# State space stage of a fused layer kernel: scan tiles of four states by 32 channels

## The chip, the cores and the metric

The kernel runs on one core of one Trainium2 chip. The metric is the device time of one execution, in microseconds (us); lower is better. The median of the runs before the change is 4260.15 us (4258.0 to 4260.63, 3 runs).

## The reference

Six parts follow each other on `x` of shape 16 x 512 x 256 (batch, time, features): a quantised feed-forward half step, a selective state space step, the feed-forward half step again, a LoRA half step, a causal attention, a LoRA half step. The change is in the state space step alone, which is this, for each batch:

```python
xz = layernorm(x) @ W_in;  x, z = split(xz)              # 512 x 512 each
x  = silu(conv(x) + conv_b)                              # 4 taps along time, per channel; called u below
proj = x @ W_x;  dt_low, Bm, Cm = proj[:16], proj[16:32], proj[32:]
dt = softplus(dt_low @ W_dt + b_dt);  A = -exp(A_log)    # A: 512 channels x 16 states
h_t = exp(dt_t * A) * h_(t-1) + (dt_t * x_t) * Bm_t      # 512 channels x 16 states, 512 times
y_t = sum over states of h_t * Cm_t
out = ((y + x * D) * silu(z)) @ W_out
```

## The kernel before

The state space stage is `mamba_phase`. Time lies along the free axis, channels along the 128 partitions. A batch is 32 steps (`STEPS`): four chunks `c` of 128 channels, and in each chunk eight steps `k` of two states. I write s0 to s31 for the steps of a batch, s = 8c + k. One step does this:

- POOL (`make_bx`, called two steps ahead): `bx` = dt*u times a row of B. Three buffers.
- ACT (`factors`, called one step ahead): two Exp of 511 elements into `da`, a PSUM tile, two buffers.
- VectorE (DVE): one `tensor_tensor_scan` over 128 x 1024 elements (both states in a row) into `h`. `h` lies in PSUM with one buffer; for two `k` of eight (`other`) it lies in SBUF as `hs`, and POOL makes `g` instead of DVE.
- DVE or POOL: `g` = h times a row of C.
- TensorE (PE, `accumulate`): adds `g` of both states to `y`, one PSUM bank, by two 128x128 matmuls with the identity; the first of a chunk adds u*D before. Float32 matmuls of 512 columns are two instructions each.
- At the end of a chunk, `finish_mult` on DVE multiplies `zs` (silu of z) by `y`.

The rows of B and C come over DRAM: the projection goes to `bd`, and `fetch` loads one `bc` tile of 128 x 2048 for each `k` with a broadcast over the 128 partitions (1 MB, eight a batch, in chunk 3 of the batch before). `dt` and `dt*u` stay in SBUF, in tiles of their own.

While a batch is scanned, a Python generator, `prepare(b + 1)`, makes the next batch's inputs, one piece per step: transposes, input projections, conv taps, `w_x`, `w_dt`, z. Its PSUM tile `mm` has one buffer, so that a piece goes PE, ACT, PE, ACT. The conv works on `stacks` (`xs`): ACT copies a projected chunk to `xp`, one DMA stores it to DRAM (`xc`), four DMAs load it to 32 partitions each (`xs`), each shifted by one time step, and `taps(c)` folds them by matmuls of 128x32 into four groups of 32 output partitions. For chunk 3 of the next batch, `taps(3)` is PE's piece of s13 and its bias (`to_u(3)`) ACT's piece of s14.

Each engine runs its instructions in the order written (`keep_in_program_order`); DMAs all go on SP's queue, in an order that the framework's scheduler decides, and SP waits there for the buffer and the data of one DMA before it looks at the next. The framework gives DMAs eight semaphores in turn, so a DMA also waits for the eighth before it.

Of the kernel before, what the change touches and what calls it, by code (L numbers as in the profile page):

```python
# [16 lines left out]
P = 128  # L17
# [8 lines left out]
NS = 16  # L26
# [10 lines left out]
def macaron_kernel(  # L37
# [365 lines left out]
    def mamba_weights(mw):  # L403
        w = {}
        w["in"] = mw.tile([P, KD, 2 * DI], F32, name="w_in")
        nc.sync.dma_start(out=w["in"], in_=W_in.rearrange("(k p) f -> p k f", p=P))

        w_x = mw.tile([P, NDC, P], F32, name="w_x")
        nc.gpsimd.memset(w_x, 0.0)
        wx_src = W_x.rearrange("(c p) f -> p c f", p=P)  # L410
        for i in range(3):
            nc.sync.dma_start(
                out=w_x[:, :, 32 * i : 32 * i + 16],
                in_=wx_src[:, :, 16 * i : 16 * (i + 1)],
            )
# [13 lines left out]
        a_neg = mw.tile([P, NDC, NS], F32, name="a_neg")  # L429
        nc.sync.dma_start(out=a_neg, in_=A_log.rearrange("(c p) n -> p c n", p=P))  # L430
# [12 lines left out]
        nc.gpsimd.tensor_tensor(fold, ident[:, :32], ident[:, 32:64], op=ALU.add)  # L443
        for i in range(2, 4):
            nc.gpsimd.tensor_tensor(
                fold, fold, ident[:, 32 * i : 32 * i + 32], op=ALU.add
            )
        for c in range(NDC):
            nc.gpsimd.tensor_scalar(
                w["dskd"][:, c, :], fold, w["dsk"][:, c : c + 1], None, op0=ALU.mult  # L450
            )
            for i in range(4 * c, 4 * c + 4):
                nc.gpsimd.tensor_scalar(
                    w["cwd"][:, i, :], fold, cw[:, i : i + 1], None, op0=ALU.mult
                )

        w["taps"] = mw.tile([P, NDC, DCONV], F32, name="ct")
        nc.sync.dma_start(out=w["taps"], in_=conv_wT.rearrange("(c p) k -> p c k", p=P))
        w["xp"] = []
        for i in range(2):  # L460
            w["xp"].append(mw.tile([P, SEQ], F32, name=f"xp{i}"))

        w["xT"] = mw.tile([P, KD, SEQ], F32, name="xT")
        return w

    def mamba_phase(w, src, dst):
        with tc.tile_pool(name="m1", bufs=1) as m1, tc.tile_pool(
# [11 lines left out]
            def pool(out, in0, in1, op):  # L479
                tc.keep_in_program_order(nc.gpsimd.tensor_tensor(out, in0, in1, op=op))  # L480
# [9 lines left out]

            w_in, w_x, w_dt, w_out = w["in"], w["x"], w["dt"], w["out"]
            a_neg, dskd, cwd, xps = w["a"], w["dskd"], w["cwd"], w["xp"]
            NP = NS // 2
            STEPS = NDC * NP


# [13 lines left out]
                stacks.append(t)  # L510

            state, xns, xos, zss, rows, norms, bds = {}, {}, {}, {}, {}, {}, {}


            h0 = ps_h.tile([P, 2, SEQ], F32, name="h", tag="h")
# [17 lines left out]
                    )  # L533
                return p

            def fetch(b, k):


                if b < NB:
                    bc = m2.tile([P, 2, 2, SEQ], F32, name="bc", tag="bc", bufs=NP)  # L540
                    nc.sync.dma_start(
                        out=bc, in_=bds[b][k : k + 1].to_broadcast([P, 2, 2, SEQ])
                    )
                    rows[b, k] = bc

            def load(b):

# [53 lines left out]
            def prepare(b):  # L601
# [109 lines left out]
                bd = md.tile([NP, 2, 2, SEQ], F32, name="bd", tag="bd")  # L711
                for i in range(2):
                    nc.sync.dma_start(
                        out=bd.rearrange("k n i s -> (k n) i s")[:, i, :],
                        in_=proj[32 + 32 * i : 32 + 32 * i + NS, :],
                    )
                bds[b] = bd
                dts, dtus = [], []

                def to_dtu(h):  # L720
                    for j in range(2):
                        pool(dtus[h][:, j, :], dts[h][:, j, :], us[h][:, j, :], ALU.mult)

                for h in range(2):
                    dt = m2.tile([P, 2, SEQ], F32, name="dt", tag="dt", bufs=3)
                    dtu = m2.tile([P, 2, SEQ], F32, name="dtu", tag="dtu", bufs=3)
                    dts.append(dt)
                    dtus.append(dtu)
                    for j in range(2):
                        c = 2 * h + j  # L730
                        p = mm()
# [3 lines left out]
                        )  # L735
                        yield
                        act(
                            dt[:, j, :], p, AF.Identity, bias=w["bdt"][:, c : c + 1]
                        )
                        if h and j == 0:  # L740
                            to_dtu(0)
                    yield
                    act(dt, dt, AF.Softplus)
                state[b] = (us, dts, dtus)
                scale = norm_scale(b + 1)
                next(scale, None)
                yield "scan"
# [58 lines left out]
            def make_bx(t):  # L806
                b, c, k = where(t)
                if b < NB:
                    bx = m2.tile([P, 2, SEQ], F32, name="bx", tag="bx", bufs=3)
                    dtu = state[b][2][c // 2][:, c % 2 : c % 2 + 1, :]  # L810
                    pool(
                        bx, dtu.to_broadcast([P, 2, SEQ]), rows[b, k][:, :, 0, :], ALU.mult
                    )
                    bxs[t] = bx

            def accumulate(b, c, k, g):
                if k == 0:
                    ys.append(ps_y.tile([P, SEQ], F32, name="y", tag="y"))
                    u = state[b][0][c // 2][:, c % 2, :]
                    for i in range(0, P, 32):  # L820
                        pe(
                            ys[0][i : i + 32, :], lhsT=dskd[i : i + 32, c, :],
                            rhs=u[i : i + 32, :], start=True, stop=False,
                        )
                for j in range(2):
                    pe(
                        ys[0], lhsT=ident, rhs=g[:, j, :], start=False,
                        stop=(k == NP - 1 and j == 1),
                    )
                if k == NP - 1:  # L830
                    done.append((b, c, ys.pop()))

            def flat(t):
# [3 lines left out]
            for n, got in enumerate(rest):  # L837
# [3 lines left out]
                        pass  # L841
                if got:
                    break
            for k in range(NP):
                fetch(0, k)
            spare.clear()
            for t in range(2):
                make_bx(t)
            def factors(t):

                b, c, k = where(t)
                if b < NB:
                    for j in range(2):
                        n = 2 * k + j
                        act(
                            das[t % 2][:, j, 1:], state[b][1][c // 2][:, c % 2, 1:],
                            AF.Exp, scale=a_neg[:, c, n : n + 1],
                        )

            factors(0)  # L860
            due = {}
            for t in range(STEPS * NB):
                b, c, k = where(t)
                s = t % STEPS
# [3 lines left out]
                make_bx(t + 2)  # L868
                factors(t + 1)

                other = k % 4 == 1
                if other:
                    h = m2.tile([P, 2, SEQ], F32, name="hs", tag="hs", bufs=1)
                else:
# [4 lines left out]
                ))  # L879


                for args in reversed(due.pop(t, ())):
                    accumulate(*args)
                if s == 8:
                    load(b + 2)
                if 16 <= s < 24:
# [1 line left out]

                for _ in range(2 if t < 8 else 1):
                    next(rest if t < 4 else ahead, None)  # L890
                g = m2.tile([P, 2, SEQ], F32, name="g", tag="g", bufs=4)
                C = rows[b, k][:, :, 1, :]
# [4 lines left out]
                due.setdefault(t + 1 + other, []).append((b, c, k, g))  # L897
# [7 lines left out]
            for args in due.pop(STEPS * NB):  # L905
                accumulate(*args)
# [829 lines left out]
```

## Time and profile before

| | |
|---|---|
| median of 3 runs | 4260.15 us |
| span of the profiled execution | 4259.0 us |
| state space stage, first to last scan | 617.5 to 2429.3 us of the span, 512 scans |
| DMA share in this stage | 0.39 to 0.49 |
| PE, DVE, ACT, POOL busy, window 1000 to 1100 us | 89.4, 93.0, 73.6, 88.0 us |

The page gives the span of the profiled execution; the runs' times lie about 1 us above it. The page's columns: a group of instructions is given by its line, engine and operation, with the tiles it writes and reads, the number, the busy time, the mean of one, and the idle time just before them with what ended it. A matmul is recorded with its weight load (PEld) apart. PEclk is the share of full clock that TensorE was granted. Shares over the whole span mix stages; this stage is 43% of it.

### The profile page before, as it was taken

The page shows a single profiled execution, that of the slowest core. Times are in us where ns is not written, and L with a number is a line of the kernel's source. Part 1 is how long each engine was busy: PE and PEld are TensorE (multiplying, and loading weights), DVE is VectorE, ACT ScalarE, POOL GpSimd, SP SyncE. Part 2 cuts the span into 40 slices and gives each one's busy share as a digit, 9 for nine tenths or more (in the row PEclk, how much of TensorE's full clock was granted, in tenths as well). Part 3 has the DMA queues.
Part 4 walks back from the last instruction along what each step waited for, and adds up shares of the span by engine and source line. Part 5 has one row for each costly group of instructions (what it writes and reads, how often), then busy time and mean ns, then how long its engine had stood idle before and what let it go on. Part 6 is the DMA issues. An engine that isn't in the chain of part 4 may idle for free.

```text
span 4259.0 us, 50441 instructions
## 1 busy us (share of the span) xinstructions
PE 3903.6 (92%) x17986; PEld 2129.9 (50%) x17986; DVE 3751.8 (88%) x4970; ACT 2284.9 (54%) x3463; POOL 1877.2 (44%) x1653
## 2 busy tenths in 40 slices
PE   6999977988899888888888799999999999999989
PEld 4676632333333333333333366666755555555547
DVE  9999858999999999999999899998878888888766
ACT  4444336667767676676777344443524444444434
POOL 1000027888888898888988600000301111111121
PEclk9999999999999999999999999999999999999999
DMA  4000023444444444444443020000000000000002
GB/s 143 16 16 15 20 100 104 132 122 134 139 144 144 144 143 144 134 135 133 139 138 120 11 109 1 1 1 1 13 21 20 19 17 18 19 20 14 21 11 70
DMA packets 120605, 303.00 MB, mean 71 GB/s; under 512 B 25297, under 2 KB 45330, under 8 KB 103970
## 3 DMA queue, kind: packets, MB, share of 16 engines
q1 hardware_dynamic: 120354, 299.78, 22.4%
q8 instruction: 142, 2.33, 0.2%
q14 instruction: 109, 0.89, 0.1%
HBM read 238.63 MB, written 44.30 MB: 66 GB/s over the span
## 4 chain that ended last, share of the span: by engine, by line
PE 66%; DVE 14%; POOL 12%; ACT 5%; issue 2%; DMA 1%; SPq 0%; DVEq 0%; POOLq 0%; ACTq 0%
PE y L486 11%; PE s L1065 10%; PE g L288 7%; PE u L288 7%; POOL bx L480 7%; PE o L324 7%; PE p L486 5%; PE p L1065 4%; DVE h L876 4%; PE o L486 3%; PE p L1068 3%; PE o L1065 3%; POOL g L480 2%; PE r L1065 2%; DVE mx L1196 2%
## 5 line engine op out<-in xcount | busy, mean ns | idle before, releaser
L480 POOL TENSOR_TENSOR bx<-dtu,bc 128x1024 f32<-128x1024 f32 x512 | 1193.9, 2360 | 46.4 <-DVE h L876 46.3
L486 PE MATMUL y<-g,ident 128*128 128x512 f32 x2048 | 1008.9, 631 | 128.7 <-DVE g L483 128.6
L876 DVE TENSOR_TENSOR_SCAN h<-da,bx 128x1024 f32<-128x1024 f32 x384 | 879.8, 2291 | 67.8 <-ACT da L477 30.4
L477 ACT ACTIVATE da<-dt,a_neg 128x511 f32<-128x511 f32 x1024 | 702.9, 688 | 219.3 <-DVE hs L876 116.8
L486 PEld LDWEIGHTS y<-g,ident 128*128 128x128 f32 x2048 | 390.0, 199 | 711.4 <-issue 464.8
L1242 POOL TENSOR_SCALAR_AFFINE_SELECT eT<-eT 128x256 f32<-128x256 f32 (+1 forms) x384 | 189.0, 492 | 867.0 <-ACT eT L1236 867.0
L1236 ACT ACTIVATE eT<-s 128x768 f32<-128x768 f32 (+1 forms) x384 | 338.4, 881 | 422.1 <-PE s L1065 422.1
L483 DVE TENSOR_TENSOR g<-h,bc 128x1024 f32<-128x1024 f32 x384 | 468.9, 1221 | 28.2 <-PE o L486 0.5
L1065 PE MATMUL s<-k,q 32*128 32x256 f32 (+3 forms) x2048 | 458.2, 469 | 9.1 <-DVE mx L1196 5.7
L1196 DVE TENSOR_REDUCE mx<-s 128x2 f32<-128x1024 f32 (+3 forms) x512 | 410.2, 822 | 12.5
L1065 PE MATMUL s<-qm,k 32*128 32x512 f32 (+3 forms) x2048 | 385.5, 471 | 18.2 <-ACT eT L1236 11.8
L480 POOL TENSOR_TENSOR g<-hs,bc 128x1024 f32<-128x1024 f32 x128 | 301.6, 2356 | 156.8 <-DVE hs L876 140.8
L1192 DVE TENSOR_TENSOR s<-s,mask 128x256 f32<-128x256 f32 (+1 forms) x384 | 199.0, 518 | 155.7 <-PE s L1065 145.6
L293 ACT ACTIVATE sl<-g 128x352 f32<-128x352 f32 x256 | 118.1, 464 | 383.2 <-PE g L288 372.4
L876 DVE TENSOR_TENSOR_SCAN hs<-da,bx 128x1024 f32<-128x1024 f32 x128 | 292.0, 2281 | 2.5 <-ACT da L477 2.5
L1065 PEld LDWEIGHTS s<-k,q 32*128 32x128 f32 x2048 | 205.7, 184 | 172.2 <-issue 93.8
L1393 POOL TENSOR_TENSOR g<-rs,v 128x4 f32<-128x4 f32 x64 | 13.1, 208 | 631.8 <-ACT rs L1390 548.8
L486 PE MATMUL p<-xT,w_in 128*128 128x512 f32 x500 | 242.1, 607 | 20.9 <-ACT xT L477 10.1
L509 POOL MEMSET xs<- 128x12 f32 x2 | 0.2, 110 | 532.7 <-DMA xd<-x 532.7
L477 ACT ACT_TABLE_LOAD x170 | 218.1, 1283 | 3.0
L1065 PEld LDWEIGHTS s<-qm,k 32*128 32x128 f32 x2048 | 170.1, 185 | 63.9 <-ACT eT L1236 34.7
L288 PE MATMUL g<-wgT,xT 128*128 128x352 f32 x512 | 183.7, 469 | 0.0
(270 smaller groups left out, 6766.6 us busy)
## 6 DMA issues: line engine op xcount, KB each, us to landing
bc<-bd SPq DMA_DIRECT2D x128, 1024.0 KB, 6.3
xs<-xc SPq DMA_DIRECT2D x240, 256.0 KB, 4.7
xc<-xp SPq DMA_DIRECT2D x60, 256.0 KB, 2.0
x<-_attn_hidden_states_dram SPq DMA_DIRECT2D x16, 512.0 KB, 6.6
xd<-x SPq DMA_DIRECT2D x16, 512.0 KB, 2.6
xo<-xd SPq DMA_DIRECT2D x16, 512.0 KB, 3.6
xe<-xo SPq DMA_DIRECT2D x16, 512.0 KB, 2.6
x<-xe SPq DMA_DIRECT2D x16, 512.0 KB, 10.7
```

What stands on the lines that cost most here:

```text
L288: nc.tensor.matmul(dst, lhsT=xT[:, k, c * P : (c + 1) * P], rhs=w[:, k, f0 : f0 + HF], start=(k == 0), stop=(k == KD - 1),)
L324: last = nc.tensor.matmul(o, lhsT=hT[:, f, :], rhs=wdT[:, f, :], start=(f == 0), stop=False)
L477: return tc.keep_in_program_order(nc.scalar.activation(out, in_, func, **kw))
L480: tc.keep_in_program_order(nc.gpsimd.tensor_tensor(out, in0, in1, op=op))
L483: tc.keep_in_program_order(nc.vector.tensor_tensor(out, in0, in1, op=op))
L486: tc.keep_in_program_order(nc.tensor.matmul(out, **kw))
L876: tc.keep_in_program_order(nc.vector.tensor_tensor_scan(flat(h), flat(das[t % 2]), flat(bxs.pop(t)), 0.0, op0=ALU.mult, op1=ALU.add,))
L1065: tc.keep_in_program_order(nc.tensor.matmul(out, **kw))
L1192: nc.vector.tensor_tensor(own, own, const["mask"][:, :w].unsqueeze(1).to_broadcast([P, 2, w]), op=ALU.add)
L1196: nc.vector.tensor_reduce(mx[:, t, 2 * pair : 2 * pair + 2, RM], s[:, :, off : off + (t + 1) * P], axis=AX.X, op=ALU.max,)
L1236: const["exp"] = nc.scalar.activation(eT[:, 2 * pair : 2 * pair + 2, e0 : e0 + w], s[:, :, :w], AF.Exp)
L1242: nc.gpsimd.affine_select(out=own, in_=own, compare_op=ALU.is_ge, fill=0.0, base=0, pattern=[[0, 2], [0, n], [1, P]] if n > 1 else [[0, 2] ...
```

## The change

A scan tile now holds four states by 32 channels on its partitions, and two groups of 32 channels one after the other on the free axis; the scan's size stays. The step count stays 32 a batch: `q = k // 2` chooses the states (partition group i has state 4i + q), `p = k % 2` the pair of channel groups.

- `dt` and `dt*u` are made in one tile as before, stored to DRAM (`dd`, 1 MB for two chunks, two a batch) and loaded back by `fetch_steps`: for each chunk two tiles `ds` of 128 x 2048, each by four DMAs of 32 partitions (256 KB) that read the same data. Four buffers.
- The B and C rows: `bc` has 128 x 1024 elements, four tiles a batch, each by four DMAs of 32 partitions (128 KB). Five buffers instead of eight.
- `y`: the `g` of a pair of steps are added by four matmuls with `fold` (128x32, four stacked identities), each to 32 partitions of `y`. Before: four of 128x128 for two steps.
- `other` is now k % 4 == 0 (k = 0, 4), before k % 4 == 1 (k = 1, 5). `g` has five buffers, before four.
- `A_log` is loaded by four DMAs instead of one, in the new order.

```diff
@@ mamba_weights
+        a_neg = mw.tile([P, 4 * NDC, 4], F32, name="a_neg")
+        for i in range(4):
+            nc.sync.dma_start(
+                out=a_neg[32 * i : 32 * i + 32],
+                in_=A_log.rearrange("(g m) n -> m g n", m=32)[:, :, 4 * i : 4 * i + 4],
+            )
...
@@ mamba_phase
+            def fetch(b, q):
                 if b < NB:
+                    bc = m2.tile([P, 2, SEQ], F32, name="bc", tag="bc", bufs=5)
+                    for i in range(4):
+                        n = 4 * i + q
+                        nc.sync.dma_start(
+                            out=bc[32 * i : 32 * i + 32],
+                            in_=bds[b][n : n + 1].to_broadcast([32, 2, SEQ]),
+                        )
+                    rows[b, q] = bc
+            def fetch_steps(b, c):
+                if b < NB:
+                    rows_of = steps_of[b, c // 2][c % 2].rearrange(
+                        "(g m) x s -> m g x s", m=32
+                    )
+                    for p in range(2):
+                        t = m2.tile([P, 2, 2, SEQ], F32, name="ds", tag="ds", bufs=4)
+                        for i in range(4):
+                            nc.sync.dma_start(
+                                out=t[32 * i : 32 * i + 32],
+                                in_=rows_of[:, 2 * p : 2 * p + 2],
+                            )
+                        spread[b, c, p] = t
...
                 def to_dtu(h):
+                    t = dts[h]
                     for j in range(2):
-                        pool(dtus[h][:, j, :], dts[h][:, j, :], us[h][:, j, :], ALU.mult)
+                        pool(t[:, j, 1, :], t[:, j, 0, :], us[h][:, j, :], ALU.mult)
+                    dd = md.tile([2, P, 2, SEQ], F32, name="dd", tag="dd", bufs=4)
+                    nc.sync.dma_start(out=dd.rearrange("j p x s -> p j x s"), in_=t)
+                    steps_of[b, h] = dd
...
                     pool(
-                        bx, dtu.to_broadcast([P, 2, SEQ]), rows[b, k][:, :, 0, :], ALU.mult
+                        bx, spread[b, c, k % 2][:, :, 1, :],
+                        B.to_broadcast([P, 2, SEQ]), ALU.mult,
                     )
...
-            def accumulate(b, c, k, g):
+            def accumulate(b, c, q, gs):
...
-                for j in range(2):
+                for i in range(4):
                     pe(
-                        ys[0], lhsT=ident, rhs=g[:, j, :], start=False,
-                        stop=(k == NP - 1 and j == 1),
-                    )
+                        ys[0][32 * i : 32 * i + 32, :], lhsT=fold,
+                        rhs=gs[i // 2][:, i % 2, :], start=False, stop=(q == NQ - 1),
+                    )
...
                     for j in range(2):
+                        g = 4 * c + 2 * p + j
                         act(
+                            das[t % 2][:, j, 1:], spread[b, c, p][:, j, 0, 1:],
+                            AF.Exp, scale=a_neg[:, g, q : q + 1],
                         )
...
-                other = k % 4 == 1
+                other = k % 4 == 0
...
+                pair.append(g)
+                if k % 2:
+                    due[t + 1] = (b, c, k // 2, pair)
+                    pair = []
                 if k == 0 and done:
                     finish_mult(*done.pop())
-                if s >= STEPS - NP:
-                    fetch(b + 1, k)
+                if k == 1 and c < NDC - 1:
+                    fetch_steps(b, c + 1)
+                if k == 2 and c == NDC - 1:
+                    fetch_steps(b + 1, 0)
+                if k % 2 and c == NDC - 1:
+                    fetch(b + 1, k // 2)
```

More of the change, by code (lines that the diff above doesn't have):

```diff
@@ L428, in mamba_weights @@
             )
-        a_neg = mw.tile([P, NDC, NS], F32, name="a_neg")
-        nc.sync.dma_start(out=a_neg, in_=A_log.rearrange("(c p) n -> p c n", p=P))
+        a_neg = mw.tile([P, 4 * NDC, 4], F32, name="a_neg")
[4 more added lines that the diff above has]
+            )
         nc.scalar.activation(a_neg, a_neg, AF.Exp)
@@ L447, in mamba_weights @@
             )
+        w["fold"] = fold
         for c in range(NDC):
@@ L492, in mamba_phase @@
             a_neg, dskd, cwd, xps = w["a"], w["dskd"], w["cwd"], w["xp"]
+            fold = w["fold"]
             NP = NS // 2
+            NQ = NP // 2
             STEPS = NDC * NP
@@ L512, in mamba_phase @@
             state, xns, xos, zss, rows, norms, bds = {}, {}, {}, {}, {}, {}, {}
+            spread, steps_of = {}, {}
             h0 = ps_h.tile([P, 2, SEQ], F32, name="h", tag="h")
@@ L534, in in_proj @@
                 return p
-            def fetch(b, k):
+            def fetch(b, q):
                 if b < NB:
-                    bc = m2.tile([P, 2, 2, SEQ], F32, name="bc", tag="bc", bufs=NP)
-                    nc.sync.dma_start(
-                        out=bc, in_=bds[b][k : k + 1].to_broadcast([P, 2, 2, SEQ])
-                    )
-                    rows[b, k] = bc
+                    bc = m2.tile([P, 2, SEQ], F32, name="bc", tag="bc", bufs=5)
[10 more added lines that the diff above has]
+                        "(g m) x s -> m g x s", m=32
+                    )
+                    for p in range(2):
[6 more added lines that the diff above has]
+                        spread[b, c, p] = t
             def load(b):
@@ L710, in prepare @@
                 act(proj, p, AF.Copy)
-                bd = md.tile([NP, 2, 2, SEQ], F32, name="bd", tag="bd")
+                bd = md.tile([NS, 2, SEQ], F32, name="bd", tag="bd")
                 for i in range(2):
                     nc.sync.dma_start(
-                        out=bd.rearrange("k n i s -> (k n) i s")[:, i, :],
+                        out=bd[:, i, :],
                         in_=proj[32 + 32 * i : 32 + 32 * i + NS, :],
@@ L717, in prepare @@
                 bds[b] = bd
-                dts, dtus = [], []
+                dts = []
                 def to_dtu(h):
+                    t = dts[h]
                     for j in range(2):
-                        pool(dtus[h][:, j, :], dts[h][:, j, :], us[h][:, j, :], ALU.mult)
+                        pool(t[:, j, 1, :], t[:, j, 0, :], us[h][:, j, :], ALU.mult)
+                    dd = md.tile([2, P, 2, SEQ], F32, name="dd", tag="dd", bufs=4)
+                    nc.sync.dma_start(out=dd.rearrange("j p x s -> p j x s"), in_=t)
+                    steps_of[b, h] = dd
                 for h in range(2):
-                    dt = m2.tile([P, 2, SEQ], F32, name="dt", tag="dt", bufs=3)
-                    dtu = m2.tile([P, 2, SEQ], F32, name="dtu", tag="dtu", bufs=3)
+                    dt = m2.tile([P, 2, 2, SEQ], F32, name="dt", tag="dt", bufs=2)
                     dts.append(dt)
-                    dtus.append(dtu)
                     for j in range(2):
@@ L737, in prepare @@
                         act(
-                            dt[:, j, :], p, AF.Identity, bias=w["bdt"][:, c : c + 1]
+                            dt[:, j, 0, :], p, AF.Identity, bias=w["bdt"][:, c : c + 1]
                         )
@@ L742, in prepare @@
                     yield
-                    act(dt, dt, AF.Softplus)
-                state[b] = (us, dts, dtus)
+                    act(dt[:, :, 0, :], dt[:, :, 0, :], AF.Softplus)
+                state[b] = us
                 scale = norm_scale(b + 1)
@@ L809, in make_bx @@
                     bx = m2.tile([P, 2, SEQ], F32, name="bx", tag="bx", bufs=3)
-                    dtu = state[b][2][c // 2][:, c % 2 : c % 2 + 1, :]
+                    B = rows[b, k // 2][:, :1, :]
                     pool(
-                        bx, dtu.to_broadcast([P, 2, SEQ]), rows[b, k][:, :, 0, :], ALU.mult
+                        bx, spread[b, c, k % 2][:, :, 1, :],
+                        B.to_broadcast([P, 2, SEQ]), ALU.mult,
                     )
                     bxs[t] = bx
-            def accumulate(b, c, k, g):
-                if k == 0:
+            def accumulate(b, c, q, gs):
+                if q == 0:
                     ys.append(ps_y.tile([P, SEQ], F32, name="y", tag="y"))
-                    u = state[b][0][c // 2][:, c % 2, :]
+                    u = state[b][c // 2][:, c % 2, :]
                     for i in range(0, P, 32):
@@ L824, in accumulate @@
                         )
-                for j in range(2):
+                for i in range(4):
                     pe(
-                        ys[0], lhsT=ident, rhs=g[:, j, :], start=False,
-                        stop=(k == NP - 1 and j == 1),
+                        ys[0][32 * i : 32 * i + 32, :], lhsT=fold,
+                        rhs=gs[i // 2][:, i % 2, :], start=False, stop=(q == NQ - 1),
                     )
-                if k == NP - 1:
+                if q == NQ - 1:
                     done.append((b, c, ys.pop()))
@@ L843, in mamba_phase @@
                     break
-            for k in range(NP):
-                fetch(0, k)
+            fetch_steps(0, 0)
+            for q in range(NQ):
+                fetch(0, q)
             spare.clear()
@@ L852, in factors @@
                 if b < NB:
+                    q, p = k // 2, k % 2
                     for j in range(2):
-                        n = 2 * k + j
+                        g = 4 * c + 2 * p + j
                         act(
-                            das[t % 2][:, j, 1:], state[b][1][c // 2][:, c % 2, 1:],
-                            AF.Exp, scale=a_neg[:, c, n : n + 1],
+                            das[t % 2][:, j, 1:], spread[b, c, p][:, j, 0, 1:],
+                            AF.Exp, scale=a_neg[:, g, q : q + 1],
                         )
             factors(0)
-            due = {}
+            due, pair = {}, []
             for t in range(STEPS * NB):
@@ L879, in mamba_phase @@
                 ))
-                for args in reversed(due.pop(t, ())):
-                    accumulate(*args)
+                if t in due:
+                    accumulate(*due.pop(t))
                 if s == 8:
@@ L890, in mamba_phase @@
                     next(rest if t < 4 else ahead, None)
-                g = m2.tile([P, 2, SEQ], F32, name="g", tag="g", bufs=4)
-                C = rows[b, k][:, :, 1, :]
+                g = m2.tile([P, 2, SEQ], F32, name="g", tag="g", bufs=5)
+                C = rows[b, k // 2][:, 1:, :].to_broadcast([P, 2, SEQ])
                 if other:
@@ L896, in mamba_phase @@
                     vec(g, h, C, ALU.mult)
-                due.setdefault(t + 1 + other, []).append((b, c, k, g))
+                pair.append(g)
+                if k % 2:
+                    due[t + 1] = (b, c, k // 2, pair)
+                    pair = []
                 if k == 0 and done:
                     finish_mult(*done.pop())
-                if s >= STEPS - NP:
-                    fetch(b + 1, k)
+                if k == 1 and c < NDC - 1:
[4 more added lines that the diff above has]
+                    fetch(b + 1, k // 2)
                 if s == STEPS - 1:
@@ L904, in mamba_phase @@
                         pass
-            for args in due.pop(STEPS * NB):
-                accumulate(*args)
+            accumulate(*due.pop(STEPS * NB))
             finish_mult(*done.pop())
```

## The prediction

> **What bounds the kernel now.** I read the page first, then the windows and waits of the scan stage, then one batch instruction by instruction. The change touches only the scan stage: 512 steps, 617 to 2432 us, 112.6 us a batch in the mean of batches 1 to 14 (from the starts of their scans). The page's groups show its main loads (mean ns behind the busy time):
>
> ```profile
> L480 POOL TENSOR_TENSOR bx<-dtu,bc 128x1024 f32<-128x1024 f32 x512 | 1193.9, 2360 | 46.4 <-DVE h L876 46.3
> L486 PE MATMUL y<-g,ident 128*128 128x512 f32 x2048 | 1008.9, 631 | 128.7 <-DVE g L483 128.6
> L876 DVE TENSOR_TENSOR_SCAN h<-da,bx 128x1024 f32<-128x1024 f32 x384 | 879.8, 2291 | 67.8 <-ACT da L477 30.4
> L483 DVE TENSOR_TENSOR g<-h,bc 128x1024 f32<-128x1024 f32 x384 | 468.9, 1221 | 28.2 <-PE o L486 0.5
> ```
>
> A batch has 32 scans, 24 `g` on DVE, 4 `zs` and the statistics: 107.6 us of DVE work, 109.4 with the pipeline's short gaps. So DVE sets the pace and only about 3 us a batch are waits. The waits between 1000 and 1948 us (8.4 batches; total, times, longest) say which:
>
> ```profile
> DVE zs L483 <- PE y L486: 20.8, 9, 3.2
> DVE h L876 <- ACT da L477: 3.2, 11, 0.3
> DVE h L876 <- POOL bx L480: 2.8, 7, 0.4
> ```
>
> The first is one stall a batch, 2.3 us in the mean, at s8: PE is late with `y` because the pieces of `prepare` and the `y` sums share it. Here it is, on DVE's timeline, where `zs` waits from 1228.35 to 1231.55:
>
> ```profile
> 1227.12 1.23 DVE L483 TENSOR_TENSOR g<-h,bc 128x1024 f32<-128x1024 f32 x1
> 1231.55 0.69 DVE L483 TENSOR_TENSOR zs<-zs,y 128x512 f32<-128x512 f32 x1 [3.20 <-PE y L486]
> ```
>
> However light PE gets, no more than 3 us in 112.6 can be won. Lateness on the other engines can cost without such a bound.
>
> **PE.** Four full matmuls for two steps are 8 instructions at 0.43 us, 3.44 us. Four 128x32 ones are what the conv taps run: 1.06 us for 8. That is 16 x 2.4 = 38 us of PE a batch. It is worth only the `zs` wait: 0 to 2.3 us. I take 1.3, since at s8 a projection (1.88 us) still stands in front of the sum, later than before (below), and `zs` now comes after a scan of 2.2 us instead of scan and `g` (3.5 us). 14 x 1.3 = -18; batch 0, -2.
>
> **Unchanged.** POOL's `bx` and `g`, ACT's Exp and DVE's work keep count and size; the operand that is repeated changes sides. Four `A_log` DMAs instead of one end hundreds of us before `a_neg` is used, while POOL idles. I take 0 for both; if `bx` did slow by 1%, POOL's cover of 7 us a batch would hide it outside the stretch below.
>
> **The start.** The first `bx` began at 614.55, when `dt*u` was done. Now `dd` (1 MB) is stored and the first `ds` loaded before it. The stores `xe<-xo` and `xd<-x` of half that size land after 2.9 and 2.6 us, so about 4; four 32-partition loads take 6.0 from first issue to last landing (`xs`, below). Together +10, nothing beside it. The second `ds` may hold scan 1 by 2 more.
>
> **DMA order.** DMA volume grows little (8 MB of `bc` become 2 of `bc`, 8 of `ds`, 2 of `dd`), at a share of 0.4 to 0.5. The order on SP matters more. In the built kernel the queue of a batch reads:
>
> ```
> ... xc(2), ds x1, xs(2) x4, ds x7, xc(3), xe, ds x1, xs(3) x4, ds x5, bd ...
> ```
>
> Before, nothing stood between `xc(3)` and `xs(3)`. The single `ds` in front of `xs(3)` fills a buffer of chunk 1, whose last readers are `bx` and `da` of s14. `da` of s14 overwrites the `da` of s12, so it runs after the scan of s12. Behind that wait sit `xs(3)`, then `taps(3)` on PE, `to_u(3)` on ACT, and the `da` that DVE needs at s16. SP before, with 3.6 us from `xc(3)` to `xs(3)`:
>
> ```profile
> 1237.79 0.34 SPq L647 DMA_DIRECT2D xc<-xp  x1
> 1241.40 1.73 SPq L650 DMA_DIRECT2D xs<-xc  x4
> ```
>
> `taps(3)` followed at 1250.39, 9 us after. ACT then has little left:
>
> ```profile
> 1251.52 0.69 ACT L477 ACTIVATE u<-p,cb 128x512 f32<-128x512 f32 x1 [0.92 <-PE p L486]
> 1252.11 1.41 ACT L477 ACTIVATE da<-dt,a_neg 128x511 f32<-128x511 f32 x2
> 1253.53 1.28 ACT L477 ACT_TABLE_LOAD   x1
> 1254.82 1.06 ACT L477 ACTIVATE u<-u 128x1024 f32<-128x1024 f32 x1
> 1255.90 1.28 ACT L477 ACT_TABLE_LOAD   x1
> ```
>
> Count from the start of scan s12. It ends at 2.3, `da` s14 ends at 3.75, the `ds` is issued by 4.2. `xs(3)` takes 6.0 (last packet of four, 16 groups of four batches: 5.8 to 6.4) plus 0.3 to 0.9 for the `ds` in front: 10.5 to 11.1. `taps(3)`: 1.06, or 1.84 as at 659.24. `u` 0.69, `da` 1.41: 13.7 to 15.0. DVE wants it at 2.20 + 3.66 + 3.69 + 3.54 = 13.1. Then two table loads, Silu and `da`, 5.03 us, against 3.33 until scan s17 (scan, `zs`, statistics): 1.7 more. So 2.3 to 3.6 us a batch.
>
> The low end with a warm PE and a faster load: 2.1. The high end: `xc(3)` itself lands late. It queues behind 7 `ds` of 256 KB, which on one row move as fast as `bc` (430 GB/s, 0.6 us each) and on another as `xs` (about 205 GB/s, 1.3 us each). At the slow rate it lands up to 4.3 us after SP's wait: 8 us. I take 3.3, the slow PE with the `ds` in front, nearest to the `xs` rows. 15 batches prepare a next one: 15 x 3.3 = +50. Below nothing isn't possible for this term: no engine waits less for it.
>
> The clock of PE enters here. The same taps group took 1.84 us after PE had idled 4.7 us, and 1.06 in a dense stretch:
>
> ```profile
> 659.24 1.84 PE L486 MATMUL p<-xs,cwd 128*32 128x512 f32 x8 [4.71 <-DMA xs<-xc]
> 1250.39 1.06 PE L486 MATMUL p<-xs,cwd 128*32 128x512 f32 x8
> ```
>
> [...]
>
> **POOL's order.** With `other` at k = 0, 4 the `g` of s28 comes before `bx` s31; before, that of s29 came after it. POOL's tightest stretch starts when scan s20 ends and frees a `bx` buffer:
>
> ```profile
> 1273.26 2.35 POOL L480 TENSOR_TENSOR bx<-dtu,bc 128x1024 f32<-128x1024 f32 x1 [1.50 <-DVE h L876]
> ...
> 1304.30 2.35 POOL L480 TENSOR_TENSOR bx<-dtu,bc 128x1024 f32<-128x1024 f32 x1
> ```
>
> From 1273.26 to the end of `bx` s31 at 1306.65 are 33.4 us; one more `g` (2.31 spacing) makes 35.7. DVE's steps from s20 to s31 sum to 36.3, of which 2.25 are scan s20, so it wants `bx` s31 after 34.1: a stall of 1.6, against 0.39 at the next scan before. +1.3; 15 x 1.3 = +20. Bounds: -0.4 (the old stall gone) to 1.7 a batch.
>
> **Other DMA waits.** `xo` is now loaded only about 15 us into a batch, the loads for `taps(0)` come some 3 us later than PE could use them. ACT's slack covers both by about 2 us at s8 to s10; without that cover it is the `zs` stall that stays, which I counted half. The first `ds` of the next batch lands about 6 us before its `bx`.
>
> **The sum.** 4259.0 + 10 - 18 - 2 + 50 + 20 = 4319, and with 1.15 between the profiled span and the median, 4320.
>
> **The rivals.**
>
> 1. Faster: the conv path isn't late. It decides whether `xs(3)` lands within 8.1 us of the start of scan s12 (then even s17 is on time). For it: ACT and PE run ahead when PE is light. Against: SP's wait ends at 3.75 and no `xs` group took under 5.8. Price: no 50, the `zs` stall and the ACT wait all gone (14 x 2.7 = 38), POOL 0 to 20: 4259 + 10 - 38 - 2 + 0 to 20, plus 1.15: 4230 to 4250.
> 2. Much slower: loads to 32 partitions run at the slow rate, `xc(3)` is late each time. For: the last three of four `xs` DMAs took 0.17 us for a packet of 2 KB, the first 0.084. Against: their rows are 2060 bytes apart, `ds` rows are not. 15 x 5.5 to 8 = 82 to 120, `zs` not gained, POOL 20: 4370 to 4410.
> 3. No difference: the terms cancel, 4252 to 4269 (within 0.2%, about what a measurement of this kernel can tell).
> 4. The fold matmuls don't overlap in their column groups. Then the sums cost PE what they did, -18 goes: 4338. Against: the taps row, 8 in 1.06 us. It lies in the forecast's range.
>
> **Chances.** Forecast (4270 to 4370, with 4) 0.57, rival 1 0.14, rival 2 0.22, rival 3 0.07. Faster 0.14, same 0.07, slower 0.79. The range leaves out most of rival 1 below and the upper end of rival 2: 4255 to 4390.
>
> **What would show it.** Right: no `zs` wait at s8 over 2 us; DVE waits for ACT `da` at s16 and s17, 2 to 4 us a batch; PE waits for `xs` before `taps(3)`; SP's L565 waits for ACT; POOL `bx` stalls DVE at s31; first scan near 627; batches of about 115.5 us. Wrong: batches of 110 us (rival 1), `ds` landing times over 8 us (rival 2), or slower POOL or DVE operations, which I excluded.

## The result, and the profile after

| | before | after |
|---|---|---|
| median, us | 4259.07 (4 runs, 4257.65 to 4260.63) | 4394.68 (4 runs, 4392.38 to 4396.41) |
| ratio to before | 1 | 1.0318, 95% interval 1.0304 to 1.0333 |
| span of the profiled execution | 4259.0 | 4390.6 |
| first scan | 617.5 | 630.2 |
| batch 0 | 129.4 | 142.1 |
| batches 1 to 14, mean | 112.63 | 120.65 |
| mean granted clock of TensorE | 0.975 | 0.894 |

The change costs 3.2%. Of the 131.6 us between the spans, 12.6 are the start, 12.7 batch 0 and 14 x 8.02 = 112 the batches after it; batch 15 and the stages behind give about 6 back. The groups of the changed kernel, with the columns of before:

```profile
L485 POOL TENSOR_TENSOR bx<-ds,bc 128x1024 f32<-128x1024 f32 x512 | 1195.1, 2355 | 136.0 <-DVE h L906 121.7
L491 PE MATMUL y<-g,fold 128*32 128x512 f32 x2048 | 485.7, 768 | 280.5 <-DVE g L488 199.7
L906 DVE TENSOR_TENSOR_SCAN h<-da,bx 128x1024 f32<-128x1024 f32 x384 | 880.6, 2293 | 88.1 <-POOL bx L485 30.6
L491 PE MATMUL p<-xs,cwd 128*32 128x512 f32 x480 | 79.5, 727 | 184.3 <-DMA xs<-xc 169.5
```

POOL's `bx` and DVE's scan cost per instruction what they did (2360 and 2291 ns before). The folded sums take PE 486 us instead of 1009, so the edit does what it says, and the matmuls of the four groups overlap (2048 of 768 ns in 486 us); it is 33 us a batch, where 38 were reckoned. The last line shows where PE waits instead: of 184.3 us of idle time before the conv taps, a DMA (`xs`) ends 169.5. DVE's waits in the same window as before, 1000 to 1948 us:

```profile
DVE hs L906 <- ACT da L482: 52.1, 16, 5.0
DVE h L906 <- POOL bx L485: 14.2, 8, 1.9
DVE zs L488 <- PE y L491: 12.8, 12, 1.4
DVE h L906 <- ACT da L482: 10.6, 8, 1.7
```

I sorted every gap of over 0.15 us in front of a DVE instruction by its step and took the mean over batches 1 to 14. Waits rose from 3.14 to 11.27 us a batch, 8.1 more, which is what a batch grew by. The table has them in us a batch (blank: under 0.1). The expectations below name some of them by the step before: their s7 and s8 are s8 here, their s15 and s16 are s16 and s17, and s30 is s31.

| kernel | median, us | ratio to before | batch 1-14 | s0 | s4 | s8 | s14 to s17 | s31 |
|---|---|---|---|---|---|---|---|---|
| before | 4259.1 | | 112.63 | 0.38 | | 2.30 | 0.30 | |
| after | 4394.7 | 1.0318 | 120.65 | | | 3.22 | 6.20 | 1.72 |
| pool_order_back | 4383.9 | 1.0295 | 120.36 | 0.55 | | 3.63 | 7.34 | |
| interleaved | 4363.3 | 1.0249 | 118.71 | | | 2.75 | 4.79 | 1.71 |
| queue_pinned | 4381.8 | 1.0291 | 120.18 | | | 1.93 | 7.12 | 1.71 |
| order_early_ds | 4388.1 | 1.0309 | 120.07 | | 2.76 | 0.27 | 5.87 | 1.73 |
| all_mended | 4257.3 | 0.9999 | 111.88 | 0.53 | | | 2.35 | |
| all_mended_xs | 4254.0 | 0.9992 | 111.39 | 0.54 | | | 1.90 | |
| c2_at_s1 | 4217.3 | 0.9908 | 109.45 | 0.53 | | | | |
| split_bc_before | 4438.4 | 1.0426 | 124.78 | 0.32 | | 6.83 | 8.35 | |
| half_y_before | 4254.1 | 0.9994 | 112.57 | 0.35 | | | 3.02 | |
| before_pinned | 4254.1 | 0.9994 | 112.64 | 0.38 | | 2.30 | 0.31 | |
| before_pinned_xs | 4252.6 | 0.9990 | 112.65 | 0.38 | | 2.30 | 0.31 | |
| before_pinned_half_y | 4208.3 | 0.9884 | 109.66 | 0.35 | | | | |

The largest item, s16 and s17, is the conv path that the prediction named. Batch 4 of the changed kernel, SP, then PE, ACT and DVE; scan s12 starts at 1176.17:

```profile
1173.12 0.34 SPq L672 DMA_DIRECT2D xc<-xp  x1
1178.39 0.34 SPq L817 DMA_DIRECT2D xe<-xo  x1
1179.96 0.32 SPq L565 DMA_DIRECT2D ds<-dd  x1
1181.69 1.74 SPq L675 DMA_DIRECT2D xs<-xc  x4
```

```profile
1189.45 1.93 PE L491 MATMUL p<-xs,cwd 128*32 128x512 f32 x8 [9.96 <-DMA xs<-xc]
```

```profile
1191.44 0.69 ACT L482 ACTIVATE u<-p,cb 128x512 f32<-128x512 f32 x1 [9.35 <-PE p L491]
1192.03 1.41 ACT L482 ACTIVATE da<-ds,a_neg 128x511 f32<-128x511 f32 x2
```

```profile
1193.54 2.29 DVE L906 TENSOR_TENSOR_SCAN hs<-da,bx 128x1024 f32<-128x1024 f32 x1 [4.05 <-ACT da L482]
```

Read it backwards: DVE is idle from 1189.5 to 1193.5 for a `da`, which stands on ACT behind `u`; `u` waits for `taps(3)`, PE for `xs(3)`. That group is issued from 1181.69, and PE can start 7.8 us later. Its issue waited for the single `ds` and then for the landing of `xc(3)`, a store of 256 KB that had been on the queue since 1173.12, behind seven `ds` loads.

### The profile page after: what moved, and what is told of

The parts are those of the page before. It is cut to its first block, busy times and chain, and to the rows that moved or that the text cites. A ratio compares the mean times of both kernels' runs of the same rounds, so it can differ in the third digit from the quotient of the medians.

```text
span 4390.6 us, 51755 instructions
## 1 busy us (share of the span) xinstructions
PE 3555.1 (81%) x17986; PEld 1844.6 (42%) x17986; DVE 3752.9 (85%) x4970; ACT 2289.4 (52%) x3463; POOL 1878.2 (43%) x1653
## 4 chain that ended last, share of the span: by engine, by line
PE 50%; DVE 15%; DMA 14%; POOL 8%; ACT 6%; issue 4%; SPq 2%; DVEq 0%; POOLq 0%; ACTq 0%
PE s L1101 10%; PE g L288 7%; PE u L288 7%; PE o L324 7%; DVE h L906 5%; DMA xs<-xc 5%; POOL bx L485 5%; PE p L1101 4%; DMA xc<-xp 3%; DMA ds<-dd 3%; PE p L1104 3%; PE o L1101 3%; PE p L491 2%; DVE g L488 2%; ACT da L482 2%
## 5 line engine op out<-in xcount | busy, mean ns | idle before, releaser
L485 POOL TENSOR_TENSOR bx<-ds,bc 128x1024 f32<-128x1024 f32 x512 | 1195.1, 2355 | 136.0 <-DVE h L906 121.7
L906 DVE TENSOR_TENSOR_SCAN h<-da,bx 128x1024 f32<-128x1024 f32 x384 | 880.6, 2293 | 88.1 <-POOL bx L485 30.6
L482 ACT ACTIVATE da<-ds,a_neg 128x511 f32<-128x511 f32 x1024 | 705.0, 689 | 329.5 <-DVE h L906 241.4
L491 PE MATMUL y<-g,fold 128*32 128x512 f32 x2048 | 485.7, 768 | 280.5 <-DVE g L488 199.7
L1232 DVE TENSOR_REDUCE mx<-s 128x2 f32<-128x1024 f32 (+3 forms) x512 | 410.1, 822 | 12.5
L491 PE MATMUL p<-xT,w_in 128*128 128x512 f32 x500 | 274.9, 676 | 86.8 <-ACT zs L482 48.3
L491 PEld LDWEIGHTS y<-g,fold 128*32 128x32 f32 x2048 | 67.0, 123 | 643.7 <-DVE g L488 375.5
L491 PE MATMUL p<-xs,cwd 128*32 128x512 f32 x480 | 79.5, 727 | 184.3 <-DMA xs<-xc 169.5
L491 PEld LDWEIGHTS p<-xT,w_in 128*128 128x128 f32 x500 | 94.9, 211 | 283.9 <-issue 91.1
```

Of the source, the lines that this page charges most:

```text
L482: return tc.keep_in_program_order(nc.scalar.activation(out, in_, func, **kw))
L491: tc.keep_in_program_order(nc.tensor.matmul(out, **kw))
L906: tc.keep_in_program_order(nc.vector.tensor_tensor_scan(flat(h), flat(das[t % 2]), flat(bxs.pop(t)), 0.0, op0=ALU.mult, op1=ALU.add,))
L1232: nc.vector.tensor_reduce(mx[:, t, 2 * pair : 2 * pair + 2, RM], s[:, :, off : off + (t + 1) * P], axis=AX.X, op=ALU.max,)
```

## Experiments

The theory from the two traces: the 32-partition `ds` and `bc` loads are slow (256 KB of `ds` land 7.3 us after their issue, where 1 MB of `bc` took 6.3 before), and everything queued behind them is late. Rivals: SP's waits and the order of the queue; POOL's order; PE's lower clock.

**pool_order_back** gives POOL's `g` its old place in the chunk.

```diff
-                other = k % 4 == 0
+                other = k % 4 == 1
-                    due[t + 1] = (b, c, k // 2, pair)
+                    due[t + 1 + other] = (b, c, k // 2, pair)
```

> The changed kernel with POOL's share as before: other is k % 4 == 1 again, and the pair that holds POOL's g is added two steps later instead of one. If the g of s28 in front of bx s31 is what holds scan s31 (1.7 us in 14 batches of the changed kernel, step s30 at 5.39 instead of 3.7), that stall goes and at most 0.4 us comes back at the next scan: 15 x 1.3 to 1.7 = 20 to 26 us, about 4370. The other stalls (s7, s8, s15, s16) stay as they are. Rival: POOL is late by its load, not by its order; then the stall moves to another step and the time stays within 5 us of 4394.

Measured: 4383.89 us, 1.0295 (1.028 to 1.0311), between the theory's number and the rival's. The wait at s31 is gone, as reckoned (0.55 is left, at s0), but a batch is only 0.3 us shorter: s16 waits 1.1 longer, s8 0.4. I read this so: while the conv path sets the pace, a wait removed elsewhere comes back in front of it. Half of the 10 us between the two spans lie in the start (3.3) and in batch 0 (1.8).

**interleaved** puts state group i on partitions i, i + 4, i + 8 ... The bytes, the number of DMAs and their sizes stay.

```diff
-                                out=t[32 * i : 32 * i + 32],
+                                out=t[i::4],
-                            out=bc[32 * i : 32 * i + 32],
+                            out=bc[i::4],
```

(and `fold` and `a_neg` in the same order)

> The changed kernel with the states interleaved on the partitions: state group i lies on partitions i, i + 4, i + 8 and so on, so each DMA to 32 partitions covers the whole height of SBUF instead of a block; fold and the order of A follow. Number, size and order of the DMAs are unchanged. Theory (destination): loads of 32 adjacent partitions run at half rate because they all end in one quarter of SBUF; then packets of 4 KB take about 0.16 us instead of 0.28 to 0.33, ds lands in about 5 us instead of 7.3, xc(3) lands before SP's wait for da of s14 ends, and the stalls at s15 and s16 fall from 6.3 us a batch to the 2.3 to 3.6 that the wait alone gives: 15 x 3 = 45, about 4350. Rival (form): the rate comes from the number of partitions of a DMA or from reading the same rows four times; then packets and time stay: 4394.

Measured: 4363.31 us, 1.0249 (1.0232 to 1.0267). The median packet of 4 KB took 159 ns, in the changed kernel 295. The page's DMA issues (size of one, median us from issue to landing), first of the changed kernel, then of this one:

```profile
ds<-dd SPq DMA_DIRECT2D x512, 256.0 KB, 7.3
```

```profile
ds<-dd SPq DMA_DIRECT2D x512, 256.0 KB, 4.8
```

So the target's partitions alone halve the time of a packet. This holds for loads that follow each other: the packets of the single `ds` in front of `xs(2)` took 159 ns (median; 64 of them a batch) in the changed kernel too. Why a load by itself is spared, no run shows.

A batch still waits 4.8 us at s16 and s17, more than the 2.3 to 3.6 expected. `xc(3)` now lands 2.9 us after the start of scan s12, and `xs(3)` is issued at 4.5 (means of batches 1 to 14), right behind the `ds` that waits for `da` of s14. But `xs(3)`, still in the slow form, lands only 7.6 us after that.

**queue_pinned** keeps every DMA of the stage in the written order, loads `xo` as soon as the last `xe` is stored, and at the start one `bc` ahead of the first `ds`; the slow form stays.

```diff
+            def dma(out, in_):
+                tc.keep_in_program_order(nc.sync.dma_start(out=out, in_=in_))
...
                     dma(out=dst[b], in_=xos.pop(b))
+                    load_xo(b + 1)
```

> The changed kernel with the stage's DMAs pinned in the order in which they are written, with xo of the next batch loaded right after the store of xe, and with bc of q = 0 ahead of the first ds. So no ds of chunk 3 stands in front of xs(3), but the ds of chunk 2 still stand in front of xc(3). The stalls at s7 and s8 (3.1 us a batch), which I put down to the late xo, should go: 15 x 3 = 45. For the stalls at s15 and s16 (6.3 us): if SP's wait is their cause, they fall under 2 us, about 4285; if the rate of the 7 ds ahead of xc(3) is, xs(3) lands only about 1.3 us sooner and 5 us are left, about 4330.

Measured: 4381.84 us, 1.0291 (1.0276 to 1.0307), neither of the two numbers. DVE no longer waits for ACT at s8 (1.86 of the 3.22 in the changed kernel), and PE's wait for `xo` is gone from its list, so that part was the late `xo`; `zs` waits 1.93 there instead of 1.36. The conv path is worse, 7.12: now all eight slow `ds` of a chunk stand right in front of `xc(3)`, which lands 7.6 us after the start of scan s12, in the changed kernel 6.3.

**order_early_ds** has the edit of queue_pinned and also takes the `ds` loads away from there: six buffers, each chunk fetched one chunk ahead.

```diff
-                if k == 1 and c < NDC - 1:
-                    fetch_steps(b, c + 1)
+                if k == 5 and c < NDC - 2:
+                    fetch_steps(b, c + 2)
                 if k == 2 and c == NDC - 1:
                     fetch_steps(b + 1, 0)
+                if k == 5 and c == NDC - 1:
+                    fetch_steps(b + 1, 1)
```

> After's kernel with all DMAs of the stage kept in the written order, xo loaded a step group earlier, and ds in six buffers: the two ds tiles of a chunk are fetched one chunk ahead (s5, s13, s26, s29), so that no ds load and no wait for da stands between xc(3) and xs(3), and none is in flight when xc(3) is stored. The loads keep their slow form (32 neighbouring partitions). Theory (taps(3) is late because slow ds loads and their buffer wait are in front of xc(3) and xs(3)): the waits at s15 and s16 shrink from 6.3 us a batch to 0 to 2.5, the one at s7 is gone, those at s8 (2) and s30 (1.7) stay; batches of 113 to 116 us, 4285 to 4325 us in all. Rival (the rate alone counts, wherever the loads stand, or PE's clock): s15 and s16 keep 5 us or more, 4350 us or more.

Measured: 4388.06 us, 1.0309 (1.0295 to 1.0323), the rival's number. Its SP queue, and one of DVE's waits in the window 1000 to 1948 us:

```profile
1155.83 5.48 SPq L494 DMA_DIRECT2D ds<-dd  x8
1163.38 0.34 SPq L494 DMA_DIRECT2D xc<-xp  x1
1172.05 1.74 SPq L494 DMA_DIRECT2D xs<-xc  x4
1173.89 0.38 SPq L494 DMA_DIRECT2D xc<-xp  x1
```

```profile
DVE hs L915 <- POOL bx L485: 22.5, 8, 3.4
```

The eight loads are now in front of `xc(2)`, so `xs(2)` follows it after 8.7 us and pushes `xc(3)` back in turn. A new wait appears at s4 (the line above): the next `bc` is late for POOL, 2.76 us a batch. So in both orders tried at this rate, loads in a row delay something that an engine waits for. The last order below was not tried at this rate.

**all_mended** is the same order with the interleaved layout and POOL's old order. **all_mended_xs** spreads the conv stacks too (`stacks[c % 2][k::4, ...]`, the weights to match).

> The kernel of order_early_ds, and besides: the four states lie on every fourth partition instead of in blocks of 32 (ds and bc loads at the fast rate), and POOL makes its g at k = 1 and 5 as in the kernel before. Theory (the loss is only late data and POOL's order; the folded sums and the repeated operand cost nothing by themselves): s30 has no wait, s15 and s16 at most 1 us, s8 at most 1; batches of 109.5 to 111.5 us, and with 1822 us behind the stage 627 + 136 + 14 x 110.5 + 107 + 1822 = 4239 us (4225 to 4255), below the kernel before. Rival (the lighter PE is clocked down, so that its chain for zs and taps stays late whatever the loads do): s8 and s15 keep 2 us or more, batches of 113, 4275 us or more.

> The kernel of all_mended with the conv stacks spread in the same way (tap k on every fourth partition, weights placed to match), so that the xs loads run at the fast rate too. Theory: a group of four xs loads lands in 3 to 4.5 us instead of 6; if all_mended still waits at s15, that goes; if not, the same time within 0.2%. Rival (the slowness of xs has to do with its 2 KB rows, not with neighbouring partitions): the group still takes 6 us.

Measured: 4257.31 us, 0.9999 (0.999 to 1.0008), and 4254.03 us, 0.9992 (0.9983 to 1.0). The first is 2 us above its range because 2.35 us are left at s16; the second is 3 us lower still, less than 0.1%. The packets of the `xs` loads were sped up (the median of all 2 KB packets is 84 ns instead of 146), so the gap between the rows, which the prediction had blamed, was not what made them slow. But the group of four landed 6.3 us after its first issue instead of 6.8 (means of batches 1 to 14), not 3 to 4.5: issuing the four now takes SP 2.5 us instead of 1.7 (the `xs` lines below, of c2_at_s1 and of all_mended). What is left at s16 shows in the queue of all_mended:

```profile
1119.54 5.64 SPq L499 DMA_DIRECT2D ds<-dd  x8
1125.27 0.53 SPq L499 DMA_DIRECT2D xn<-xd  x1
1125.91 0.38 SPq L499 DMA_DIRECT2D xc<-xp  x1
1131.60 1.74 SPq L499 DMA_DIRECT2D xs<-xc  x4
1133.44 0.38 SPq L499 DMA_DIRECT2D xc<-xp  x1
1138.76 1.73 SPq L499 DMA_DIRECT2D xs<-xc  x4
```

Eight `ds` and the `xn` hold `xc(2)` for 5.7 us, `xs(2)` holds `xc(3)` for 5.3.

**c2_at_s1** is all_mended_xs and fetches chunk 2 at s1, before `xc(0)`, instead of at s5.

> The kernel of all_mended_xs with one more move: the ds tiles of chunk 2 are fetched at s1 instead of s5, so that they land before xc(0) is stored and no ds load stands in front of xc(2), xs(2), xc(3), xs(3). Theory (what is left of the waits at s15 and s16, 2 us a batch, is that queue): those waits at most 0.5 us, batches of 109.5 to 110.5 us, 14 x 1.5 to 2 us less than all_mended_xs: 4226 to 4236 us. Rival (the rest is PE clocked down or ACT's own chain): the same as all_mended_xs within 0.2%, 4245 to 4262.

Measured: 4217.34 us, 0.9908 (0.9894 to 0.9921): faster than both kernels, and below the expected range, in part because batch 0 fell as well (133.3 to 128.7). From `xc(2)` and `xc(3)` to their `xs` it is 2.5 and 2.1 us now (the lines are of `xc(3)`), and DVE's list of waits is one line and 0.7 us in all besides:

```profile
1117.35 0.33 SPq L499 DMA_DIRECT2D xc<-xp  x1
1119.42 2.52 SPq L499 DMA_DIRECT2D xs<-xc  x4
```

```profile
DVE h L920 <- POOL bx L490: 4.4, 8, 0.6
```

TensorE's mean clock here is 0.912, near the changed kernel's 0.894, so the lower mean clock is not what made the batches long. It cost where PE came last: `taps(3)`, which waited for `xs(3)`, took 1.93 us in the changed kernel, at a granted clock of 0.50 (1189.45 to 1191.38 us), and takes 1.07 here, 0.9 of the 6.2 us at s16 and s17.

**split_bc_before** is the kernel before with each 1 MB `bc` load split into four DMAs of 32 partitions; nothing else is written differently.

```diff
-                    nc.sync.dma_start(
-                        out=bc, in_=bds[b][k : k + 1].to_broadcast([P, 2, 2, SEQ])
-                    )
+                    for i in range(4):
+                        nc.sync.dma_start(
+                            out=bc[32 * i : 32 * i + 32],
+                            in_=bds[b][k : k + 1].to_broadcast([32, 2, 2, SEQ]),
+                        )
```

> The kernel before, with each 1 MB broadcast load of bc split into four loads of 32 neighbouring partitions, same bytes: the price of the form alone. Theory (a load to 32 neighbouring partitions runs at half the rate): the packets of bc take twice as long, 8 MB a batch take about 39 us instead of 20, and what stands behind them in the queue at the start of the next batch comes later; 0 to 40 us more. Rival (the rate of ds comes from something else, as its source in DRAM, read four times): packets as long as before, no change.

Measured: 4438.36 us, 1.0426 (1.0407 to 1.0445), far beyond the 40 us that I allowed. A packet of 8 KB took 618 ns (median) instead of 309: the split alone doubles the time of a packet, with another source than that of `ds`. DVE's largest wait, and PE's largest on data (none of PE's waits in the kernel before is on a DMA in this window):

```profile
DVE zs L483 <- PE y L486: 85.1, 15, 9.3
```

```profile
PE p L486 <- DMA xs<-xc: 61.3, 15, 5.6
```

PE does exactly the work of before here; at s8 its `y` is late because the taps in front of it wait for `xs`. But not all of the 4.3% is the rate. Eight loads a batch have become 32, and the scheduler made another queue: the store `xe` now stands in front of `xs(3)`, and SP waits there for ACT's copy into `xo`. Batch 4:

```profile
1173.52 0.34 SPq L649 DMA_DIRECT2D xc<-xp  x1
1182.23 0.34 SPq L792 DMA_DIRECT2D xe<-xo  x1
1182.69 2.18 SPq L652 DMA_DIRECT2D xs<-xc  x4
```

In means of batches 1 to 14, `xc(3)` lands as early as in the kernel before (1.3 us ahead of the start of scan s12 against 1.4), yet `xs(3)` is issued 5.2 us after that start, in the kernel before 1.4 ahead of it. In both kernels `xe` is issued 4.8 us after it; only its place differs. So the wait at s16 (8.0 us a batch) comes mainly from the order, and what the rate alone costs this kernel isn't shown.

**The value of a lighter PE.** half_y_before leaves out the `y` matmuls of the second state of each step (1.7 us of PE less for two steps, 27 us a batch). Its result, above the expected range, says little: here too the scheduler moved the `xe` store in front of `xs(3)`, and in place of the wait at s8 there was one of 3.0 us at s16. So it was made again on a kernel whose queue is pinned.

```diff
-                for j in range(2):
+                for j in range(1):
                     pe(
-                        stop=(k == NP - 1 and j == 1),
+                        stop=(k == NP - 1),
```

> The kernel before the change, with the y sum of the second state of each step left out, so that PE has 55 us a batch of work less 27 and nothing else changes. It measures what lighter work on PE alone is worth: by the waits of the profile before no more than about 3 us of 112.6 a batch, 2.3 of it the zs wait at s8; 14 x 2.3 to 3 plus some of the waits of batch 0: 4210 to 4228. Rival: PE's lateness hides more than the wait table shows; then batches fall under 109 us and the time under 4200.

> The kernel before with all DMAs of the stage kept in the written order and xo loaded earlier, nothing else: a base for the next two. Theory (its one wait, at s8, is PE's load, not a DMA): the wait at s8 stays near 2.3 us, 4250 to 4262 us. Rival (the wait at s8 is a late xo): it goes, 4220 to 4235.

> The kernel of before_pinned with the conv stacks spread on every fourth partition. It asks what part of a gain of c2_at_s1 the kernel before could have without four states to a tile. Theory (before has no wait on xs): within 0.2% of before_pinned. Rival: 14 us less or more, as the waits at s15 and s16 of before (0.4 us) and at s13 (0.4) go.

> The kernel of before_pinned with the y matmuls of the second state of each step left out: 16 x 1.7 = 27 us of PE a batch less and every other thing the same. It gives the value of a lighter PE alone. Theory (the wait at s8 is worth 2.3 us a batch and nothing takes its place): 14 x 2.3 less than before_pinned, 4220 to 4232. Rival (another wait, or a lower clock, takes its place): within 0.2% of before_pinned.

Measured: half_y_before 4254.13 us, 0.9994 (0.9985 to 1.0004); before_pinned 4254.11, 0.9994 (0.9985 to 1.0003); before_pinned_xs 4252.56, 0.999 (0.9981 to 0.9999); before_pinned_half_y 4208.3, 0.9884 (0.9869 to 0.9899). Pinning and spreading bring the kernel before 3 and 5 us, about 0.1%, so the gain of c2_at_s1 isn't theirs. A lighter PE alone is worth 4254.11 - 4208.3 = 46 us, more than expected: 2.98 a batch, the whole wait at s8 and most of the small ones. The clock fell with PE's work, from 0.977 to 0.941, and cost nothing that shows. These 46 us are about the ceiling of what this change could win (27 us of PE a batch less here, 33 in the change), and c2_at_s1 is 40 us below the kernel before (4257.52 to 4217.34).

## Why the prediction was wrong

The direction was right, and so were the places of the two waits that the sum added, the conv path's and POOL's. The conv path was sized at half of what came, and the gain at `zs` had the wrong sign. 4394.68 lies 4.7 us above the range and 75 above the number. It is the second rival, to which I gave 0.22 (4370 to 4410, `zs` not gained), that took place. Its sign, `ds` landing times over 8 us, showed in part: the median is 7.3, the last of a row of seven took 9.3.

- **The conv path: the step that failed.** Predicted 3.3 us a batch, with 2.1 to 8 as bounds; measured 6.2: 2.9 too little. In means of batches 1 to 14, from the start of scan s12: the `ds` was issued at 3.8 (reckoned 4.2), `xs(3)` from 6.4 instead of about 4.5, since `xc(3)` landed only at 6.3; `xs(3)` landed at 13.6 (10.5 to 11.1), and `da` was ready at 17.9 (13.7 to 15.0). The order and the wait were read rightly from the built queue. Two sizes were wrong. First, the choice between two rows for the rate, 430 GB/s of `bc` and 205 of `xs`: I let the queue in front of `xc(3)` cost nothing, on the ground that the slow `xs` rows lie 2060 bytes apart. That is the 1.9 us of `xs(3)`'s late issue. The run interleaved shows it: with fast `ds` loads `xs(3)` is issued at 4.5, as reckoned, and the wait falls from 6.2 to 4.8. Second, the time of `xs(3)` itself: I counted 6.0 to its last packet, and it took 7.2 from the first issue to the landing that PE waits for, 7.6 in interleaved (6.7 in the kernel before). This is most of why 4.8 and not 3.3 is left there; what makes the group slower than before isn't shown.

The trait that the slow loads share is the 32 neighbouring partitions. By the time of their packets, all_mended_xs shows it for `xs` (84 ns in place of 146), interleaved for `ds` (159 in place of 295), split_bc_before for `bc` (618, in the kernel before 309).

Two answers on DMA transfer, of the changed kernel (1169 to 1178 us, a stretch of `xs` and then `ds` loads, all to 32 neighbouring partitions) and of all_mended (1124 to 1131, `ds` and then `xn`):

```profile
DMA packets 766, 2.01 MB, mean 223 GB/s; under 512 B 127, under 2 KB 127, under 8 KB 766
```

```profile
DMA packets 885, 2.72 MB, mean 389 GB/s; under 512 B 157, under 2 KB 157, under 8 KB 885
```

In all_mended each `ds` load writes 32 partitions, every fourth of the 128, and the stretch with the `xn` behind them ran at 389 GB/s, against 223 with neighbouring partitions; so this rate needed no load that writes all 128. Both stretches have loads in a row: a `ds` load by itself had 159 ns a packet in either layout.

- **The `zs` wait.** Predicted 1.3 us a batch won; 0.9 lost (3.22 against 2.30). The relief of PE is worth something, 46 us by before_pinned_half_y. The cover that I named, ACT's slack over a late `xo`, wasn't there: PE waited 5 us a batch for `xo`, ACT's copy of it for PE, and the next `da` stands behind the copy. The prediction said that without this cover the `zs` stall stays; it took the other case.

```profile
PE o L491 <- DMA xo<-xd: 42.1, 8, 7.7
```

- **POOL's order.** Predicted 1.3 a batch, a wait of 1.6 in place of 0.39; measured 1.72 in place of 0.38. Right as a wait. That undoing it brings only 11 us was not foreseen: with the conv path late it is no term that adds up with the others.
- **The start.** +10, possibly 2 more; measured 12.6. Batch 0: -2 of its own, with the two terms above +2.6; measured +12.7. In c2_at_s1 batch 0 takes 128.7, so what took the waits of the later batches away took this away, too.
- **The clock** fell from 0.975 to 0.894. Each of the 15 `taps(3)` took 1.93 to 1.94 us, at a granted clock of 0.50, after 8.4 to 12.5 us without a matmul. The prediction allowed for 1.84 us, the time of one row of before (granted clock 0.54, after 4.7 us); that it would hold in every batch was the author's estimate.
- **Unchanged costs** of POOL and DVE: right, 2355 and 2293 ns.

Term by term, 10 + 2.6 + 14 x 3.3 = 59 was foreseen (here 3.3 is the whole batch: conv path 3.3, POOL 1.3, `zs` -1.3) and 12.6 + 12.7 + 14 x 8.02 - 6 = 131.6 came. Of the 4.7 us a batch between 3.3 and 8.02, 2.9 are the conv path and 2.2 the wait at s8, less 0.3 for the wait at s14 that is gone. The fixes do not add: the order alone won 7 us, the rate alone 31, POOL's order alone 11; the three together 137 (all_mended), and with the spread `xs` and the move of chunk 2 it is 177. Each alone left another late load on the same chain.

What stays open: c2_at_s1 was not run with the slow loads, so how much of its gain needs the rate and how much the order alone would bring isn't known. The 7.7 us by which its first scan is still late were not taken apart, nor were loads of 128 partitions tried, from a source already repeated in DRAM.

## What to carry to other kernels

When a change turns a full-width load into pieces, find a load in the trace that already has the new shape and take its rate, even if it differs in something else; then look at which partitions each piece writes. Here the slow loads cost through what was queued behind them (with fast `ds` loads the wait at s16 and s17 fell from 6.2 to 4.8 us a batch): follow the queue to the first transfer that an engine is waiting for. Judge an edit by its ceiling first (here 46 us by leaving the work out), and when one mended wait brings little, look for the chain that sets the period before giving the edit up.

## What the runs showed of the hardware

- Loads that follow each other, of the same size and number, had packets twice as long to 32 neighbouring partitions as to every fourth partition: 295 and 159 ns for 4 KB (after, interleaved), 146 and 84 for 2 KB (all_mended, all_mended_xs; medians of all such packets). Against a load of full width it was 618 and 309 ns for 8 KB (split_bc_before, before). A single `ds` load, 64 packets, had 159 ns also to 32 neighbouring partitions.
- Halving the time of its packets brought a group of four `xs` loads from 6.8 to 6.3 us only; issuing one of them to every fourth partition took SP 0.60 us instead of 0.42.
- split_bc_before lost 4.3%, by slower packets, more loads and another order, although DMA was busy for only 55% of the 16 engines' time in the window from 1000 to 1948 us.
